# Layer 3 of a four-layer image network: reciprocal steps folded into the transform's columns, two clipping passes, and a software pipeline over quarters of a strip

## The chip, the cores and the metric

The kernel runs on one core of a Trainium2 chip. Time is device microseconds of one execution. A core has five engines that run side by side: TensorE (PE; its weight loads are shown apart as PEld), VectorE (DVE), ScalarE (ACT), GpSimd (POOL) and SyncE (SP). In this kernel SP issues every transfer, so SP's instruction stream is one queue in which a waiting transfer holds up all that stand behind it. 16 DMA engines move the data between the chip's memory (DRAM) and the on-chip buffer SBUF; PSUM is the small memory into which PE writes.

## The reference

The network adds four layers to an input x of 2 images x 64 channels x 256 x 256 pixels, each as x = x + layer(group_norm(x)). Layers 0 to 2 are an attention over 3x3 neighbours, a pair of state-space scans, and a filtered block transform with a gated convolution. The change is about layer 3:

```
def _L3_conv_ref(x, q_table, is_encoder):       # D is the 8x8 DCT matrix
    xb = x.reshape(N, C, Hb, BLOCK, Wb, BLOCK)   # 8x8 blocks
    X = jnp.einsum('ij,ncpjqk,lk->ncpiql', D, xb, D)
    X = jnp.round(X / q)
    X = jnp.clip(X, -2 ** (BIT - 1), 2 ** (BIT - 1) - 1)
    return X.reshape(N, C, H, W)
x = x + _L3_conv_ref(_gn(x), L3_conv_q_table, 1)
```

Every 8x8 block of the normalised image is transformed, each of the 64 coefficients is divided by its own entry of q, rounded, clipped to -128..127, and added to the image. All is in float32.

## The kernel before

The image lies as 128 rows (2 images x 64 channels, one per SBUF partition) of 65,536 pixels. The four layers run one after the other; each writes its result to DRAM (y0, y1, y2, then the output) and gathers the statistics for the next layer's group norm on the way. `group_norm` ends with the multiplication that writes `gnb_l` (L177); the normalisation itself, out = scale*x + shift, is done by ACT at L191.

Layer 3 works on 32 strips of 8 image rows. A strip is one megabyte, 128 x 2048 floats. For each strip:

- SP loads it into `x3s` (L1255, three buffers), and ACT normalises it into `xn` (L191), already sorted so that 16 groups of two neighbouring 8x8 blocks lie together.
- Four times, for a quarter of a strip (four groups): PE turns the four groups round with transposes into PSUM tile `pt` (L1261), ACT copies them to `xT` (L1263), PE multiplies each with the 128x128 matrix `c_dct` (L1266) into PSUM tile `pd`, and DVE multiplies `pd` by the reciprocal of q, `rq`, into a quarter of `v` (L1269). `pt` and `pd` have three buffers each, `xT` two.
- DVE clips the whole strip (L1271) and rounds it (L1272) by adding and subtracting `RND` = 1.5 * 2^23, which leaves no room for a fraction. Both run in place on 2048 floats per partition.
- POOL adds `x3s` to `v` into `y3s` (L1274, two buffers), and SP stores it (L1275).

At the head of layer 3 the matrix and q are loaded (L1240, L1242), and DVE makes `rq` from q (L1245, L1247).

What sets the order: where the text says `tc.manual_schedule(...)` each engine executes its instructions as the program writes them; layers 1 and 2 are written so. Elsewhere, and so in layer 3, a planner orders each engine's stream at compile time by its own estimate of when each instruction can start. Waits between engines, and waits for a buffer to come free, are added automatically. Buffers of a closed pool are given to the pools opened next, so a pool's first buffers lie where the pool closed just before it had its own.

`run` calls the layers in turn. Layer 2 begins with loads of its constants (L134 for `c_fwd` and `c_inv`, then L142, L851, L858, L863) and then of its first image pieces `x2s` (L881).

Of the kernel before, what the change touches and what calls it, by code (L numbers as in the profile page):

```python
# [10 lines left out]
F32 = mybir.dt.float32  # L11
BF16 = mybir.dt.bfloat16
AF = mybir.ActivationFunctionType
ALU = mybir.AluOpType
PSUM = bass.MemoryType.PSUM
DRAM = bass.MemoryType.DRAM

P = 128
C = 64
H = W = 256  # L20
# [4 lines left out]
RND = 1.5 * 2.0**23  # L25
# [95 lines left out]
class Kernel:  # L121
# [9 lines left out]
    def load(self, name, pool=None):  # L131
        ap = self.a[name]
        t = (pool or self.const).tile(list(ap.shape), F32, name=f"t_{name}", tag=f"t_{name}")
        self.nc.sync.dma_start(t, ap)  # L134
        return t
# [1095 lines left out]
        return self.group_norm("l3", stats, count[0])  # L1231


    def layer3(self, x, y, coeffs):
        nc, tc, a = self.nc, self.tc, self.a
        xv = x.rearrange("p (h w) -> p h w", w=W)
        yv = y.rearrange("p (h w) -> p h w", w=W)
        with ExitStack() as ctx:
            keep = ctx.enter_context(tc.tile_pool(name="l3k", bufs=1))
            dct = self.load("c_dct", keep)  # L1240
            q = keep.tile([P, 8, 1, 8], F32, name="q")
            nc.sync.dma_start(  # L1242
                q.rearrange("p i o l -> p (i o l)"), a["q_table"].partition_broadcast(P)
            )
            nc.vector.reciprocal(q, q)  # L1245
            rq = keep.tile([P, 8, 8, 8], F32, name="rq")
            nc.vector.tensor_copy(rq, q.to_broadcast([P, 8, 8, 8]))  # L1247
            rq = rq.rearrange("p i n l -> p i (n l)")

            pool = ctx.enter_context(tc.tile_pool(name="l3", bufs=2))  # L1250
            p_t = ctx.enter_context(tc.tile_pool(name="l3p", bufs=3, space=PSUM))
            for s in range(H // 8):
                rows = slice(8 * s, 8 * s + 8)
                xt = pool.tile([P, 8, W], F32, name="x3s", bufs=3)
                nc.sync.dma_start(xt, xv[:, rows])  # L1255
                xn = self.affine_patches(pool, "xn3", xt, coeffs)
                v = pool.tile([P, 8, W], F32, name="v3")
                for k in range(4):
                    pt = p_t.tile([P, 4, P], F32, name="pt3")
                    for g in range(4):  # L1260
                        nc.tensor.transpose(pt[:, g], xn[:, 4 * k + g], self.ident)  # L1261
                    xT = pool.tile([P, 4, P], F32, name="xT3")
                    nc.scalar.copy(xT, pt)  # L1263
                    pd = p_t.tile([P, 8, 64], F32, name="pd3")
                    for g in range(4):
                        nc.tensor.matmul(  # L1266
                            pd[:, :, 16 * g : 16 * g + 16], xT[:, g], dct, start=True, stop=True
                        )
                    nc.vector.tensor_tensor(v[:, :, 64 * k : 64 * k + 64], rq, pd, ALU.mult)  # L1269

                nc.vector.tensor_scalar(v, v, 127.0, -128.0, ALU.min, ALU.max)  # L1271
                nc.vector.tensor_scalar(v, v, RND, RND, ALU.add, ALU.subtract)  # L1272
                yt = pool.tile([P, 8, W], F32, name="y3s")
                nc.gpsimd.tensor_add(yt, v, xt)  # L1274
                nc.sync.dma_start(yv[:, rows], yt)  # L1275

    def run(self):
        x = self.a["x"]
        coeffs = self.input_stats(x)
        layers = (self.layer0, self.layer1, self.layer2, self.layer3)  # L1280
        for i, layer in enumerate(layers):
            y = self.out if i == 3 else self.scratch(f"y{i}")
            coeffs = layer(x, y, coeffs)
            x = y


@with_exitstack
# [52 lines left out]
```

## Time and profile before

| | |
|---|---|
| median of 3 runs | 19426.9 us (19423.29 to 19428.31) |
| the profiled execution: its time / its span | 19425.37 us / 19423.1 us |
| layer 1: first normalisation | 1500.7 us |
| layer 2: first transfer of `c_fwd`, first `x2s` load, first normalisation | 15725.7, 15734.2, 15738.4 us |
| `gnb_l` of layer 3 ready | 19105.8 us |
| layer 3: first normalisation; first and last addition on POOL start | 19106.0; 19126.4 and 19413.7 us |
| last addition ends / span ends | 19418.2 / 19423.1 us |

The profile is of one execution. A line such as `L1274 POOL TENSOR_TENSOR y3s<-v,x3s` names the line of the kernel, the engine, the operation and the tiles. The columns after it are explained where lines are shown. PEclk is the granted clock of TensorE as a share of full speed. Layer 3's work on the engines in its 317 us, from the groups of instructions of the last part of the trace:

| line | engine, operation | count | busy us | mean ns |
|---|---|---|---|---|
| L1261 | PE transposes | 512 | 82.3 | 306 |
| L1266 | PE products with `c_dct` (each of the 512 is two instructions) | 1024 | 147.2 | 303 |
| L191 | ACT normalise, 128x2048 | 32 | 67.1 | 2097 |
| L1263 | ACT copy, 128x512 | 128 | 71.4 | 584 |
| L1269 | DVE multiply, 128x512 | 128 | 86.0 | 683 |
| L1271 | DVE clip, 128x2048 | 32 | 75.4 | 2356 |
| L1272 | DVE round, 128x2048 | 32 | 39.1 | 1221 |
| L1274 | POOL add, 128x2048 | 32 | 144.8 | 4524 |

### The profile page before, as it was taken

Reading aid. Unit: us, or ns where it says so; the run is one execution under the profiler, and the core shown is the slowest. Engines: PE = TensorE matmul, PEld = TensorE weight load, DVE = VectorE, ACT = ScalarE, POOL = GpSimd, SP = SyncE. Lnnn points to the kernel's source line nnn. Section 1 sums busy time; section 2 is a strip of 40 time slices with the busy share of each in tenths; the row PEclk is TensorE's granted clock in tenths of the full one; section 3 lists DMA queues with packets and bytes.
Section 4 is the critical chain, followed back from the end, with each engine's and each line's share of the span. In section 5 each row is a group of like instructions: output and inputs, shape, how many; then the busy total and the mean of one; then the engine's idle time right before and its main releaser. Section 6 shows DMA issues by size and latency. Waiting matters only on the chain. (4 is left out here: it accounts for less than half of the span.)

```text
span 19423.1 us, 164029 instructions
## 1 busy us (share of the span) xinstructions
PE 14534.9 (75%) x48720; PEld 4763.2 (25%) x48720; DVE 17991.3 (93%) x15870; ACT 12151.6 (63%) x17418; POOL 16845.3 (87%) x8646
## 2 busy tenths in 40 slices
PE   7996677767777677676677677767777679999996
PEld 3441111111111111111111111111111134444444
DVE  6888999999999999999999999999999978888896
ACT  2325666666666666666666666666666657777774
POOL 5997888888888888888888888888888878888885
PEclk9996666666666666667666666666666679999997
DMA  3116666666666666666666666666666621111104
GB/s 122 57 50 150 149 156 152 150 155 149 155 150 151 156 151 152 150 150 155 152 151 154 149 156 150 150 156 151 152 150 151 154 52 32 32 32 31 32 29 147
DMA packets 662191, 2438.92 MB, mean 126 GB/s; under 512 B 131888, under 2 KB 201264, under 8 KB 450160
## 3 DMA queue, kind: packets, MB, share of 16 engines
q1 hardware_dynamic: 661296, 2428.43, 52.1%
q8 instruction: 385, 6.31, 0.1%
q14 instruction: 510, 4.18, 0.1%
HBM read 1990.14 MB, written 437.78 MB: 125 GB/s over the span
## 5 line engine op out<-in xcount | busy, mean ns | idle before, releaser
L792 DVE TENSOR_TENSOR_SCAN h<-da,st,h 128x512 f32<-128x512 f32 x8192 | 9837.9, 1262 | 310.0 <-ACT da L789 225.5
L796 POOL TENSOR_TENSOR h<-h,cb 128x2048 f32<-128x2048 f32 x2048 | 9252.4, 4518 | 164.7 <-POOL st L795 0.2
L789 ACT ACTIVATE da<-dl,p_a 128x512 f32<-128x512 f32 x8192 | 5564.3, 688 | 3976.2 <-DVE h L792 3884.3
L561 PE MATMUL py<-h,t_c_quad 128*32 128x512 f32 x16384 | 3250.7, 817 | 1649.2 <-POOL h L796 1648.3
L561 PE MATMUL pb<-bc,t_c_sel 64*128 64x512 f32 x3072 | 2696.1, 972 | 2386.6 <-DVE h L773 2381.3
L773 DVE TENSOR_TENSOR h<-dv,pb 128x2048 f32<-128x2048 f32 x1536 | 3471.5, 2260 | 40.8 <-DMA dv<-d_dv 40.8
L1023 POOL TENSOR_TENSOR gl<-gl,prod 128x512 f32<-128x512 f32 x2056 | 2606.1, 1272 | 460.9 <-ACT prod L1019 346.7
L755 POOL TENSOR_TENSOR h<-dv,cb 128x2048 f32<-128x2048 f32 x512 | 2318.7, 4529 | 16.7 <-DMA dl<-d_dl 16.7
L982 DVE SCALAR_TENSOR_TENSOR acc<-z,tap_b,acc 128x1024 f32<-128x1024 f32 (+1 forms) x1496 | 1901.6, 1271 | 22.3
L561 PEld LDWEIGHTS pb<-bc,t_c_sel 64*128 64x128 f32 x3072 | 660.9, 267 | 4410.5 <-DVE h L773 4347.0
L1019 ACT ACTIVATE prod<-z,tap_a 128x512 f32<-128x512 f32 x2056 | 1422.3, 716 | 284.8 <-POOL gl L1023 273.8
L795 POOL COPY st<-h 128x4 f32<-128x4 f32 x2048 | 383.5, 187 | 1362.9 <-DVE h L792 1331.9
L1079 PE MATMUL pcv<-z,diag 128*128 128x512 f32 x2322 | 1236.4, 642 | 179.9 <-ACT gl L1087 166.0
L561 PEld LDWEIGHTS py<-h,t_c_quad 128*32 128x32 f32 x16384 | 423.2, 122 | 3814.4 <-POOL h L796 3222.6
L561 PE MATMUL mm<-xin,p_conv 64*128 64x512 f32 x4096 | 1318.7, 773 | 15.1 <-DMA x1t<-y 15.1
L943 PE MATMUL pz<-t_c_inv,gf 128*128 128x128 f32 (+1 forms) x8192 | 964.7, 293 | 7.6 <-ACT z L951 7.3
L561 PE MATMUL mm<-u,p_dt 128*128 128x512 f32 x1024 | 929.1, 1061 | 0.0
L943 PEld LDWEIGHTS pz<-t_c_inv,gf 128*128 128x128 f32 (+1 forms) x8192 | 792.8, 170 | 484.2 <-issue 302.5
L924 DVE TENSOR_TENSOR gf<-feff,f 128x384 f32<-128x384 f32 x1024 | 558.7, 547 | 299.9 <-PE f L915 297.4
L561 PE MATMUL py<-u,p_d 128*128 128x512 f32 x1024 | 820.9, 895 | 0.0
L951 ACT COPY z<-pz 128x512 f32<-128x512 f32 x768 | 449.7, 590 | 411.1 <-PE pz L943 330.4
L561 PEld LDWEIGHTS mm<-xin,p_conv 64*128 64x128 f32 x4096 | 459.5, 244 | 980.8 <-issue 980.6
(169 smaller groups left out, 17244.8 us busy)
## 6 DMA issues: line engine op xcount, KB each, us to landing
cb<-d_bc SPq DMA_DIRECT2D x2048, 320.0 KB
dl<-d_dl SPq DMA_DIRECT2D x2048, 256.0 KB
dv<-d_dv SPq DMA_DIRECT2D x2048, 256.0 KB
d_dl<-delta SPq DMA_DIRECT2D x256, 512.0 KB
d_dv<-du SPq DMA_DIRECT2D x256, 512.0 KB
xin<-in_x SPq DMA_DIRECT2D x16, 2048.0 KB
xt<-in_x SPq DMA_DIRECT2D x32, 1024.0 KB
y<-yt SPq DMA_DIRECT2D x128, 256.0 KB
```

The source lines that it names most:

```text
L561: nc.tensor.matmul(out, lhsT, rhs, start=start, stop=stop)
L755: nc.gpsimd.tensor_tensor(h, t["dv", b], t["cb", b][:, 0].unsqueeze(1).to_broadcast([P, 4, T]), ALU.mult,)
L773: nc.vector.tensor_tensor(h, t["dv", b], pb.unsqueeze(1).to_broadcast([P, 4, T]), ALU.mult)
L789: nc.scalar.activation(da, t["dl", b][:, k], AF.Exp, scale=ws[m]["a"][:, k, j : j + 1])
L792: nc.vector.tensor_tensor_scan(h[:, k], da, h[:, k], state[m, b][:, j, k : k + 1], ALU.mult, ALU.add)
L796: nc.gpsimd.tensor_tensor(h, h, t["cb", b][:, 1 + j].unsqueeze(1).to_broadcast([P, 4, T]), ALU.mult)
L924: nc.vector.tensor_tensor(o, feff, ph[b], ALU.mult)
L943: nc.tensor.matmul(pz[i * n : (i + 1) * n, k, :, 16 * g : 16 * g + 16], gf[t, 2 * e + g, b][:, c0 : c0 + n], inv, start=True, stop=True,)
L982: eng.scalar_tensor_tensor(out, near(s, name, m0, r, k), w, box["t"], ALU.mult, ALU.add)
L1019: nc.scalar.activation(prod, near(s, name, 4 * h + m, n, k), AF.Copy, scale=w)
L1023: nc.gpsimd.tensor_add(acc, acc, prod)
L1079: nc.tensor.matmul(box["t"], diag[:, k], near(s, f"a{i}", 4 * h + m, n, k), start=k == 0, stop=k == 8,)
```

## The change

The function `layer3` is split and rewritten.

1. A new function `layer3_weights` loads `c_dct` and q, takes q's reciprocal, and multiplies it into the columns of `c_dct`. `rq` and the multiplication at L1269 go. It is called before layer 2 starts, and its matrix lives in a pool that stays open from there to the end; q lies in a pool that is closed again before layer 2 opens its own.
2. A quarter leaves PSUM by one DVE instruction that adds `RND` and takes the minimum with `RND` + 127; one more DVE instruction per strip takes the maximum with `RND` - 128 and subtracts `RND`. Two passes over `v` (L1271, L1272) become one.
3. Every engine's order is written out. In step i, PE turns quarter i round and multiplies quarter i - 2; SP loads three strips ahead; ACT normalises the next strip between the copies of quarters 1 and 2.
4. Buffers: `x3s` 3 to 5, `xT` 2 to 4, `y3s` 2 to 3, `pt` and `pd` 3 to 4 each[...].
5. The last strip's addition is cut: rows 0 to 2 on POOL, rows 3 to 7 on DVE, with a store for each.

```
+    def layer3_weights(self, keep):
+        dct = self.load("c_dct", keep)
+        with self.tc.tile_pool(name="l3w", bufs=1) as pool:
+            q = pool.tile([P, 8, 1, 8], F32, name="q")
+            nc.sync.dma_start(
+                q.rearrange("p i o l -> p (i o l)"), a["q_table"].partition_broadcast(P)
+            )
             nc.vector.reciprocal(q, q)
-            rq = keep.tile([P, 8, 8, 8], F32, name="rq")
-            nc.vector.tensor_copy(rq, q.to_broadcast([P, 8, 8, 8]))
+            columns = dct.rearrange("p (i n l) -> p i n l", n=2, l=8)
+            nc.vector.tensor_tensor(columns, columns, q.to_broadcast([P, 8, 2, 8]), ALU.mult)
+        return dct
...
-                    nc.vector.tensor_tensor(v[:, :, 64 * k : 64 * k + 64], rq, pd, ALU.mult)
-                nc.vector.tensor_scalar(v, v, 127.0, -128.0, ALU.min, ALU.max)
-                nc.vector.tensor_scalar(v, v, RND, RND, ALU.add, ALU.subtract)
-                yt = pool.tile([P, 8, W], F32, name="y3s")
-                nc.gpsimd.tensor_add(yt, v, xt)
-                nc.sync.dma_start(yv[:, rows], yt)
...
+            def load(s):
+                if s < nstrip:
+                    xt[s] = pool.tile([P, 8, W], F32, name="x3s", bufs=5)
+                    nc.sync.dma_start(xt[s], xv[:, 8 * s : 8 * s + 8])
+            def norm(s):
+                if s < nstrip:
+                    xn[s] = self.affine_patches(pool, "xn3", xt[s], coeffs)
+            def turn(s, k):
...
+                xT[s, k] = pool.tile([P, 4, P], F32, name="xT3", bufs=4)
+                nc.scalar.copy(xT[s, k], pt)
+            def transform(s, k):
...
+                nc.vector.tensor_scalar(
+                    v[s][:, :, 64 * k : 64 * k + 64], pd, RND, RND + 127.0, ALU.add, ALU.min
+                )
+            def finish(s):
+                t = v.pop(s)
+                nc.vector.tensor_scalar(t, t, RND - 128.0, RND, ALU.max, ALU.subtract)
+                yt = pool.tile([P, 8, W], F32, name="y3s", bufs=3)
+                parts = ((nc.gpsimd, 0, 8),)
+                if s + 1 == nstrip:
+                    parts = ((nc.gpsimd, 0, 3), (nc.vector, 3, 8))
+                for eng, lo, hi in parts:
+                    eng.tensor_add(yt[:, lo:hi], t[:, lo:hi], xt[s][:, lo:hi])
+                    nc.sync.dma_start(yv[:, 8 * s + lo : 8 * s + hi], yt[:, lo:hi])
+            with tc.manual_schedule(engines={E.PE, E.DVE, E.Activation, E.Pool, E.SP}):
+                for s in range(3):
+                    load(s)
+                norm(0)
+                for i in range(4 * nstrip + 2):
+                    s, k = divmod(i, 4)
+                    if s < nstrip:
+                        if k == 0:
+                            load(s + 3)
+                        turn(s, k)
+                        if k == 1:
+                            norm(s + 1)
+                    if i >= 2:
+                        s, k = divmod(i - 2, 4)
+                        transform(s, k)
+                        if k == 3:
+                            finish(s)
...
+                if i == 2:
+                    keep = ctx.enter_context(self.tc.tile_pool(name="l3k", bufs=1))
+                    dct = self.layer3_weights(keep)
+                coeffs = layer(x, y, coeffs, *([dct] if i == 3 else []))
```

More of the change, by code (lines that the diff above doesn't have):

```diff
@@ L1231, in layer2 @@
         return self.group_norm("l3", stats, count[0])
[L1234 to L1241, printed above, removed]
+    def layer3_weights(self, keep):
+        nc, a = self.nc, self.a
+        dct = self.load("c_dct", keep)
+        with self.tc.tile_pool(name="l3w", bufs=1) as pool:
+            q = pool.tile([P, 8, 1, 8], F32, name="q")
             nc.sync.dma_start(
@@ L1245, in layer3 @@
             nc.vector.reciprocal(q, q)
-            rq = keep.tile([P, 8, 8, 8], F32, name="rq")
-            nc.vector.tensor_copy(rq, q.to_broadcast([P, 8, 8, 8]))
-            rq = rq.rearrange("p i n l -> p i (n l)")
-            pool = ctx.enter_context(tc.tile_pool(name="l3", bufs=2))
[L1251 to L1268, printed above, removed]
-                    nc.vector.tensor_tensor(v[:, :, 64 * k : 64 * k + 64], rq, pd, ALU.mult)
-                nc.vector.tensor_scalar(v, v, 127.0, -128.0, ALU.min, ALU.max)
-                nc.vector.tensor_scalar(v, v, RND, RND, ALU.add, ALU.subtract)
-                yt = pool.tile([P, 8, W], F32, name="y3s")
-                nc.gpsimd.tensor_add(yt, v, xt)
-                nc.sync.dma_start(yv[:, rows], yt)
@@ new lines, in layer3_weights, with layer3 @@
+            columns = dct.rearrange("p (i n l) -> p i n l", n=2, l=8)
+            nc.vector.tensor_tensor(columns, columns, q.to_broadcast([P, 8, 2, 8]), ALU.mult)
+        return dct
+    def layer3(self, x, y, coeffs, dct):
+        nc, tc = self.nc, self.tc
+        xv = x.rearrange("p (h w) -> p h w", w=W)
+        yv = y.rearrange("p (h w) -> p h w", w=W)
+        nstrip = H // 8
+        with ExitStack() as ctx:
+            pool = ctx.enter_context(tc.tile_pool(name="l3", bufs=2))
+            p_t = ctx.enter_context(tc.tile_pool(name="l3pt", bufs=4, space=PSUM))
+            p_d = ctx.enter_context(tc.tile_pool(name="l3pd", bufs=4, space=PSUM))
+            xt, xn, xT, v = {}, {}, {}, {}
+            def load(s):
[6 more added lines that the diff above has]
+            def turn(s, k):
+                pt = p_t.tile([P, 4, P], F32, name="pt3")
+                for g in range(4):
+                    nc.tensor.transpose(pt[:, g], xn[s][:, 4 * k + g], self.ident)
+                xT[s, k] = pool.tile([P, 4, P], F32, name="xT3", bufs=4)
+                nc.scalar.copy(xT[s, k], pt)
+            def transform(s, k):
+                pd = p_d.tile([P, 8, 64], F32, name="pd3")
+                t = xT.pop((s, k))
+                for g in range(4):
+                    nc.tensor.matmul(
+                        pd[:, :, 16 * g : 16 * g + 16], t[:, g], dct, start=True, stop=True
+                    )
+                if k == 0:
+                    v[s] = pool.tile([P, 8, W], F32, name="v3")
+                nc.vector.tensor_scalar(
[11 more added lines that the diff above has]
+                    nc.sync.dma_start(yv[:, 8 * s + lo : 8 * s + hi], yt[:, lo:hi])
+            E = mybir.EngineType
+            with tc.manual_schedule(engines={E.PE, E.DVE, E.Activation, E.Pool, E.SP}):
[5 more added lines that the diff above has]
+                    if s < nstrip:
+                        if k == 0:
+                            load(s + 3)
[7 more added lines that the diff above has]
+                            finish(s)
@@ L1280, in run @@
         layers = (self.layer0, self.layer1, self.layer2, self.layer3)
[L1281 to L1284, printed above, removed]
+        with ExitStack() as ctx:
+            for i, layer in enumerate(layers):
+                y = self.out if i == 3 else self.scratch(f"y{i}")
+                if i == 2:
+                    keep = ctx.enter_context(self.tc.tile_pool(name="l3k", bufs=1))
+                    dct = self.layer3_weights(keep)
+                coeffs = layer(x, y, coeffs, *([dct] if i == 3 else []))
+                x = y
 @with_exitstack
```

## Prediction

> **What bounds the kernel now.** I first read where layer 3 lies: from `gnb_l` at 19105.8 us to the span's end at 19423.1, 317 us or 1.6% of the span, with nothing of another layer beside it, so all of it is on the path. The first addition on POOL starts at 19126.4, the last at 19413.7: 31 strips in 287.3 us, **9.27 us a strip**. Nothing in the change touches layers 0 and 1, and layer 2 only at its start.
>
> Then the chain of work that ended last, in order of time (start, duration, what):
>
> ```profile
> 19161.91 4.51 POOL y3s L1274
> ...
> 19166.87 6.86 DMA x3s<-y
> ...
> 19173.76 2.10 ACT xn L191
> ...
> 19189.78 4.51 POOL y3s L1274
> ...
> 19194.74 6.97 DMA x3s<-y
> ```
>
> The reader is to see a ring: a strip's addition frees an `x3s` buffer, the load into it takes 6.9 us because the store issued just before it goes first, then ACT, PE, DVE and POOL follow one after another. No engine is the bound; the ring is. The waits of layer 3 say the same (who waited for whom: total us, times, longest):
>
> ```profile
> POOL y3s L1274 <- DVE v L1272: 147.0, 31, 9.7
> ...
> ACT xn L191 <- DMA x3s<-y: 77.6, 23, 6.2
> ```
>
> So each resource has room, and the question is what a strip costs when the ring is opened. Stretches of 8 us, and of 1 us around one store and load (columns: length, then busy time and instructions of PE, PEld, DVE, ACT, POOL, then granted clock, DMA share, GB/s):
>
> ```profile
> 19180.00:19188.00 8.00, 7.64 (x64) 6.92 (x63) 6.55 (x8) 5.20 (x7) 4.54 (x1) 1.00 0.05 20
> ```
>
> ```profile
> 19223.00:19224.00 1.00, 0.00 (x0) 0.00 (x0) 0.97 (x2) 1.00 (x1) 0.00 (x0) 0.50 0.95 393
> 19224.00:19225.00 1.00, 0.64 (x3) 0.64 (x4) 0.60 (x1) 0.31 (x1) 0.27 (x1) 0.50 1.13 393
> 19225.00:19226.00 1.00, 1.00 (x7) 0.93 (x5) 0.00 (x0) 0.43 (x1) 1.00 (x1) 0.50 0.99 229
> 19226.00:19227.00 1.00, 1.00 (x5) 0.80 (x4) 0.00 (x0) 0.73 (x2) 1.00 (x1) 0.50 0.91 279
> 19227.00:19228.00 1.00, 1.00 (x7) 1.00 (x6) 0.00 (x0) 0.01 (x1) 1.00 (x1) 0.50 1.01 426
> 19228.00:19229.00 1.00, 1.00 (x7) 1.00 (x6) 0.61 (x1) 0.00 (x0) 1.00 (x1) 0.50 0.89 377
> ```
>
> Last, DVE's clip beside POOL (start, duration, engine):
>
> ```profile
> 19217.74 4.51 POOL L1274 TENSOR_TENSOR y3s<-v,x3s 128x2048 f32<-128x2048 f32 x1 [2.95 <-DVE v L1272]
> 19219.59 3.75 DVE L1271 TENSOR_SCALAR v<-v 128x2048 f32<-128x2048 f32 x1
> ...
> 19223.37 1.23 DVE L1272 TENSOR_SCALAR v<-v 128x2048 f32<-128x2048 f32 x1
> ```
>
> The same kind of instruction takes 1.23 us alone and 3.75 beside an addition: it ends at 19223.34, 1.09 us after POOL's end at 19222.25. A 2048-float pass on DVE waits for POOL.
>
> **The strip after the change, by resource.**
>
> PE: 512 + 1024 instructions over 32 strips are 48 a strip, unchanged. The dense stretch above has 64 in 7.64 us, 0.119 us each: 5.73 us. [...] The row is of these float32 tiles, so I take 5.73. [...]
>
> DVE: four passes out of PSUM and one over the strip. One-source copies from PSUM took 424 ns for 256 floats (L234) and 558 for 384 (L846), so 692 for 512, as L1269 took (683): fusing the rounding costs nothing there. 4 x 0.69 + 1.22 = 3.98 us, against 6.27 before (86.0 + 75.4 + 39.1 over 32). The quarter passes read PSUM, and L1269 (672 to 690 ns throughout) shows that such passes don't wait for POOL.
>
> POOL: 4.52 us, but the strip's last DVE pass cannot run beside it: 4.52 + 1.09 + 0.13 from its end to the next addition (19224.60 to 19224.73) is a loop of 5.74 us. It needs the four quarter passes, 2.8 us, to lie beneath the addition's 4.52; if that cover goes, 2.8 us come on top.
>
> ACT: 4 x 0.584 + 2.10 = 4.43 us. Normalising stands between the copies of quarters 1 and 2; while it runs, PE has a turn, two products and another turn before it needs the next copy, some 3 us for 2.1. If a load were late, the copies behind it on ACT's queue and then PE would wait for it.
>
> DMA: 2.10 MB a strip. The six slices above move 393+393+229+279+426+377 = 2097 kB in 6.0 us: store, a dip at the change to the load (229 and 279 where 400 is usual, 0.73 us lost), load. A change from load to the next store does not occur without a gap in this trace. Bounds: no dips at all, 5.2 us; a second dip, 6.7. I take 6.0, the row itself.
>
> Does SP keep DMA fed? It issues store, load, store, load; load n stands behind the store of strip n-5, which waits for POOL, and its buffer is free then. It is wanted three strips less 7 us later (addition 4.6 us, ACT's lead 2.4): 3 x 6.1 - 7 = 11 us, where a pair lands in 6.9. So no ring closes.
>
> The largest is DMA's 6.0, with PE and POOL 0.3 behind; for waits where three so nearly agree I add 0.1. **6.1 us a strip**: 31 x (9.27 - 6.1) = 98.3 us gained.
>
> **Head of layer 3.** The loads of `c_dct` and q go, and with them the reciprocal and the wait of load 1 until 19106.8. But the first buffer of the layer's pool now lies where group norm's small tiles lay, as `c_dct` did before; SP's wait for it is in the trace:
>
> ```profile
> SPq L134 <- DVE gnb_l L177: 4.9, 1, 4.9
> ```
>
> So load 0, with all other loads behind it, starts at 19105.9 instead of 19100.6. One megabyte alone lands in some 4 us (6.9 less 2.6 for the store). Normalising then runs 19110.0 to 19112.1; PE starts at half clock (a quarter's turn 0.9 us, its product 1.8), ACT's second normalisation lies between, and the fourth product ends near 19122; with the last quarter pass and the strip pass POOL starts at 19124.0: 2.4 us gained. If load 0 is not held, 6.4.
>
> **Tail.** 768 floats on POOL (1.27 us for 512, 2.36 for 1024) take 1.82, 1280 on DVE (0.69 for 512, 2.26 for 2048) 1.48. [...]
>
> ```profile
> L430 DVE TENSOR_TENSOR part<-term,part x128: 684/689/691, 208.1 to 1448.9; 128x512 f32<-128x512 f32 x128
> ```
>
> Two SBUF inputs, minimum, median and maximum equal, though POOL's products at L356 run beside it (for instance at 706.8). Side by side: 1.95 us to POOL's end instead of 4.52, 2.6 gained; by the rule 1.2. I take 2.6. The last megabyte's stores then need the same 4.95 us as now.
>
> **Layer 2's start.** `c_dct` takes over the wait for `gnb_l` (7.0 us there too), q's load comes behind it, and `c_fwd` gets the place of q, so its load waits until DVE has multiplied q into the columns. Behind it on SP stand `c_inv`, L142, L851, L858, L863 and `x2s`, for which ACT idles 21.5 us. Least: the planner puts those ahead, and only two more issues count, 0.35 + 0.42 = 0.8 us. Most: all wait; q goes out 0.4 us after `gnb_l`, lands 4.4 us later (as in layer 3, 19106.3 to 19110.7), then the reciprocal's 0.55 and some 0.3 for the product, so `c_fwd` goes 5.7 us after `gnb_l` instead of 0.1. Nothing hides it. I take 3.
>
> **Sum.** 98.3 + 2.4 + 2.6 - 3 = 100.3 us, against the profiled execution: its span 19423.1 becomes 19322.8, and with 2.3 us around it 19325.1. The median of the runs is 1.5 above the profiled time: **19327 us** (0.51% faster).
>
> **Rivals.**
>
> *Both changes of direction dip* (15%). DMA needs 6.7 us a strip: 31 x 0.6 more, 19345 us. For it: share near 1.0 during the dip, so the engines are not idle, they are slow. Against: a change from reads to writes has no row.
>
> *DVE and POOL in convoy* (7%). If PE delivers late, quarter passes fall behind the strip pass that waits for POOL, and run after it: 4.52 + 1.22 + 4 x 0.69 = 8.5 us, 31 x 2.4 more, 19401 us, about as before. For it: DVE is one queue, and the three-strip pattern of now has such waits of 2.4 to 3.75 us. Against: four `pd` buffers let PE run a strip ahead of DVE.
>
> *PE at half clock* (4%), the slower case. Place: the whole of layer 3. At clock 0.50, 16 products took 3.78 us at 19226.2, about 0.23 us each; 48 x 0.23 = 11.0 us a strip, 31 x 4.9 more, 19479 us. It decides from 9.34 us a strip, 0.195 us an instruction. For it: layers 1 and 2 have a granted clock of 0.6 to 0.7 with PE busy two thirds of the time. Against: in layer 3 it is 1.00 in dense stretches and 0.50 only after gaps of 4.5 us and more, which go.
>
> **Chances and range.** Forecast 70%: its own range has 5.75 to 6.5 us a strip, load 0 held or not, layer 2 later by 0.8 to 5.7: 19308 to 19342. Another 4% is for smaller unnamed waits, up to 8 us a strip. 0.2% is 38.9 us, about what a measurement of this kernel can tell from no change; the convoy falls inside it. Faster 0.89, same 0.07, slower 0.04. The range 19306 to 19365 (7.3 us a strip) leaves out convoy, half clock and the rest of the unnamed.
>
> **What would show it.** DMA share in layer 3 near 0.95 and 340 GB/s instead of 0.59 and 212; PE clock near 1.00; POOL starts 6.1 us apart; the strip pass at 1.2 us; first normalisation some 4 us after `gnb_l`; in layer 2 the first `x2s` load 3 us later. POOL starts 6.7 apart with DMA share 1 speak for the first rival; DVE passes of over 2 us for the second. Wrong I would be if waits for `x3s` remain on ACT.

## The result, and the profile after

| | before | after |
|---|---|---|
| median of six runs each, us | 19426.34 (19423.29 to 19428.31) | **19306.92** (19301.38 to 19307.89) |
| ratio after / before | | **0.9938**, 95% interval 0.9926 to 0.995 |
| span of the profiled execution, us | 19423.1 | 19305.7 |

The change saves 119.4 us, 0.61%. The forecast was 19327, a gain of some 100 us; the measured median lies 1 us below the forecast's own range, 19308 to 19342. The profiled executions differ by 117.4 us in their spans, and these come from four places:

| place | before | after | gained, us | predicted |
|---|---|---|---|---|
| 31 strips, from first to last POOL addition | 287.3 (9.27 each) | 178.7 (5.77 each) | **108.6** | 98.3 |
| head: `gnb_l` to first addition | 20.6 | 18.2 | 2.4 | 2.4 |
| tail: start of last addition to end | 9.4 | 8.1 | 1.3 | 2.6 |
| all before `gnb_l` of layer 3 | 19105.8 | 19100.7 | 5.1 | -3 |

The last row holds three things: layer 2's own `gnb_l` came 1.6 later, the first normalisation after it 7.8 earlier (4.9 us instead of 12.8), and the rest of layer 2 took 1.2 longer. Of these only the second is the change. In the profiles of all kernels shown here, layer 2's `gnb_l` lies between 15725.0 and 15737.1 us, and the rest of layer 2 takes 3365 to 3370 us, though nothing was edited there. So single times are not compared below some 10 us; stages are, and, as a sum, **the stretch from layer 2's `gnb_l` to the end: 3697.4 us before, 3578.5 after**, good to some 5 us. Each experiment below but the last is a single execution, and line numbers are those of its own kernel.

The chain of work that ended last, in the kernel after (start, duration, what):

```profile
19152.64 9.78 DMA x3s<-y
19162.41 0.03 issue
19162.44 2.10 ACT xn L191
...
19169.37 0.56 ACT xT L1274
19169.93 0.01 issue
19169.93 9.62 DMA x3s<-y
```

Before, an addition by POOL stood between two loads. Now the chain passes from ACT straight to the next load and never names POOL: the old ring is open. Taken at its word, it says that loads are the bound now. The timeline of POOL and DVE in the same stretch says something else (start, duration; in brackets the idle time before, and who ended it):

```profile
19199.56 4.56 POOL L1298 TENSOR_TENSOR y3s<-v,x3s 128x2048 f32<-128x2048 f32 x1 [1.22 <-DVE v L1292]
19202.46 2.75 DVE L1292 TENSOR_SCALAR v<-v 128x2048 f32<-128x2048 f32 x1
19205.33 4.56 POOL L1298 TENSOR_TENSOR y3s<-v,x3s 128x2048 f32<-128x2048 f32 x1 [1.22 <-DVE v L1292]
19207.78 3.20 DVE L1292 TENSOR_SCALAR v<-v 128x2048 f32<-128x2048 f32 x1
19211.11 4.55 POOL L1298 TENSOR_TENSOR y3s<-v,x3s 128x2048 f32<-128x2048 f32 x1 [1.22 <-DVE v L1292]
```

The strip pass of DVE starts 2.4 to 2.9 us after the addition, would take 1.2 us, and ends at 19205.21 or 19210.98: each time 1.09 us after POOL's end (19204.12, 19209.89). POOL starts 0.12 later. The addition waits for the pass, whose result it reads, and the pass for the end of the addition before, 4.55 + 1.22 = 5.77 us, strip after strip. The waits of the end of layer 2 and of layer 3 together (who for whom: total us, times, longest):

```profile
ACT xn L191 <- DMA x3s<-y: 48.7, 22, 30.4
POOL y3s L1298 <- DVE v L1292: 37.6, 31, 1.2
```

POOL waits 1.2 us at every one of 31 strips. ACT still waits for loads, 18 us in 21 waits once the longest is taken off. And 80 us of the steady part (length, then busy us and instructions of PE, PEld, DVE, ACT, POOL, then granted clock, DMA share, GB/s):

```profile
19140.00:19220.00 80.00, 75.96 (x663) 73.78 (x663) 72.46 (x71) 56.09 (x70) 62.95 (x15) 1.00 0.99 363
```

Two resources look full, DMA by its share (0.99) and PE by its busy time (95%). Neither was the bound, as the first three experiments show.

### The profile page after: what moved, and what is told of

It reads as the page before. It is cut to its first block, busy times and chain, and to the rows that moved or that the text cites. A ratio compares the mean times of both kernels' runs of the same rounds, so it can differ in the third digit from the quotient of the medians.

```text
span 19305.7 us, 164005 instructions
## 1 busy us (share of the span) xinstructions
PE 14496.9 (75%) x48720; PEld 4739.3 (25%) x48720; DVE 17967.9 (93%) x15839; ACT 12151.6 (63%) x17418; POOL 16850.4 (87%) x8646
```

## Experiments

My theory was the loop of POOL's addition and DVE's strip pass. The rivals for the 5.77 us were DMA (the forecast's own bound) and PE.

**Which of the three: no strip pass.** The last pass over the strip is left out, and with it the clip's lower half and the subtraction of `RND`.

```
-                nc.vector.tensor_scalar(t, t, RND - 128.0, RND, ALU.max, ALU.subtract)
```

> The changed kernel without the strip pass on VectorE (the maximum with RND - 128 and the subtraction of RND are left out, so the output is not the reference's). In the changed kernel POOL's additions start 5.77 us apart. Theory 1, the loop of addition and strip pass alone is the bound: without the pass the loop is 4.55 + 0.13 = 4.7 us, and the strip falls to PE's 5.32 us (what PE took per strip where it ran without a gap): 31 x 0.45 = 14 us less in layer 3, about 19293 us. Theory 2, the DMA engines are the bound as the prediction said, or stand just behind the loop: POOL's starts stay at 5.7 to 5.8 us, the time within 3 us of the changed kernel, DMA share stays at 0.99.

Additions 5.30 us apart; `gnb_l` to end 3562.6, 15.9 less. POOL's addition and the same stretch of 80 us:

```profile
19179.28 4.55 POOL L1297 TENSOR_TENSOR y3s<-v,x3s 128x2048 f32<-128x2048 f32 x1 [0.78 <-DVE v L1286]
19184.60 4.55 POOL L1297 TENSOR_TENSOR y3s<-v,x3s 128x2048 f32<-128x2048 f32 x1 [0.77 <-DVE v L1286]
```

```profile
19140.00:19220.00 80.00, 80.00 (x724) 80.00 (x723) 41.72 (x61) 61.99 (x75) 68.38 (x16) 1.00 1.00 392
```

The same transfers run at 392 GB/s, 8% faster. A DMA share of 0.99 was therefore no sign that DMA had nothing left: 363 GB/s went with 0.99, and 392 with 1.00. PE is busy 80.00 of 80 us with 724 instructions, 0.111 us each, so 48 take 5.3 us: without the pass PE is the bound.

**Less traffic instead.** Only half of each strip is stored.

```
-                    nc.sync.dma_start(yv[:, 8 * s + lo : 8 * s + hi], yt[:, lo:hi])
+                nc.sync.dma_start(yv[:, 8 * s : 8 * s + 4], yt[:, 0:4])
```

> The changed kernel with only rows 0 to 3 of each strip stored (half of the output is left unwritten): 1.57 MB a strip instead of 2.10. Theory 1, the loop of addition and strip pass is the bound: POOL's starts stay at 5.72 us (4.54 + 1.05 + 0.13, as between the first three additions of the changed kernel), the DMA share falls to about 0.75, waits for x3s on ACT go. Theory 2, DMA is the only bound: POOL's starts fall to PE's 5.32 us or below the loop's 5.72, 31 x 0.45 = 14 us less.

```profile
19140.00:19220.00 80.00, 78.10 (x688) 76.22 (x687) 78.85 (x71) 59.35 (x71) 63.72 (x14) 1.00 0.78 277
```

Still 5.765 us a strip, with the DMA share at 0.78. A quarter of the traffic is gone, and with it ACT's waits for loads (beside the layer's first one two are left, 1.1 us together, instead of 21 with 18 us), and the time per strip does not move: those waits cost nothing.

**Both.** No strip pass and half the store.

> Both of the two: no strip pass, and half of each strip stored (output not the reference's). If loop and DMA stand side by side as bounds (the first run at 5.7 or more, the second at 5.72), only both together let the strip fall to PE's 5.32 us: about 14 us less than the changed kernel, plus some 3 us from the shorter last store. If one of them alone was the bound, this run is no faster than that one's run, but for the store.

```profile
19140.00:19220.00 80.00, 80.00 (x724) 80.00 (x723) 41.63 (x61) 62.08 (x76) 68.19 (x15) 1.00 0.84 297
```

5.290 us a strip, at 297 GB/s and with PE busy throughout: the floor without the pass is the same with three quarters of the traffic, so it is PE's and not DMA's.

**What DMA alone can do.** The loop keeps only loads and stores; each strip is stored from the buffer that it was loaded into.

```
+                for s in range(nstrip):
+                    load(s + 4)
+                    nc.sync.dma_start(yv[:, 8 * s : 8 * s + 8], xt[s])
```

> Layer 3 does nothing but load each strip and store the same buffer, four loads ahead (all its computation is left out): the cost of alternating stores and loads of 1 MB without a gap, which no row of the trace before showed. The prediction took 6.0 us a pair, 5.2 without a dip at the change of direction, 6.7 with a dip at both changes. If the changed kernel's 0.99 share in 5.77 us is saturation: 5.6 to 5.75 us a pair (365 GB/s), stores issued that far apart. If DMA had room left there: near 5.2 us (400 GB/s).

Stores went out 8.75 us apart, at 241 GB/s, slower than in the full kernel. The waits of SP's queue tell why:

```profile
SPq L1262 <- DMA out<-x3s: 217.5, 27, 12.7
```

A load into a buffer waits on SP until the store out of the same buffer has landed, 217.5 us in 27 waits, and the stores behind it on SP wait too. This measures how long a store takes to land, not what DMA can move. As a measure of the rate it failed; 392 GB/s without the strip pass is the answer that it was to give.

**How the 3.5 us a strip divide: the order alone.** The written-out order and the buffers of the changed kernel, with the arithmetic of the kernel before: quarter pass times `rq`, then two strip passes. For this q stays in the pool that is kept open, and `rq` is made at layer 3's head.

```
-                    v[s][:, :, 64 * k : 64 * k + 64], pd, RND, RND + 127.0, ALU.add, ALU.min
+                nc.vector.tensor_tensor(v[s][:, :, 64 * k : 64 * k + 64], rq, pd, ALU.mult)
...
-                nc.vector.tensor_scalar(t, t, RND - 128.0, RND, ALU.max, ALU.subtract)
+                nc.vector.tensor_scalar(t, t, 127.0, -128.0, ALU.min, ALU.max)
+                nc.vector.tensor_scalar(t, t, RND, RND, ALU.add, ALU.subtract)
```

> The changed kernel's order, buffers and early weights with the arithmetic of before: multiplication by rq out of PSUM, then two passes over the strip on VectorE, both of which wait for POOL. If the loop of addition and strip passes sets the pace, it is 5.77 + 1.22 + some 0.05 = 7.0 us a strip, so 31 x 1.25 = 39 us more than the changed kernel; the order written out is then worth 9.27 - 7.0 = 2.25 us a strip (70 us) and the arithmetic 1.25 (39 us). If the second pass hides (DMA or PE the bound), it stays at 5.8 us.

7.02 us a strip, as expected. DVE's groups by line (busy us, mean ns | idle before):

```profile
L1287 DVE TENSOR_SCALAR v<-v 128x2048 f32<-128x2048 f32 x32 | 104.5, 3265 | 1.1
...
L1288 DVE TENSOR_SCALAR v<-v 128x2048 f32<-128x2048 f32 x32 | 39.3, 1227 | 1.1
```

The first of the two passes waits for POOL, the second adds its 1.23 us to the loop. So the order and the buffers are worth 9.27 - 7.02 = 2.24 us a strip, 70 us; the arithmetic 7.02 - 5.77 = 1.26, 39 us: one strip pass less in the loop.

**Layer 2's start: the weights made late.** `layer3_weights` is called inside `layer3`, as the kernel before loaded its matrix there; q lies in the same pool as the matrix.

```
-                coeffs = layer(x, y, coeffs, *([dct] if i == 3 else []))
+                coeffs = layer(x, y, coeffs)
```

> The changed kernel with c_dct and q loaded at layer 3's head, as before, instead of ahead of layer 2. From layer 2's gnb_l to its first normalisation it took 12.8 us before and 4.9 after the change. If the early load is what shortened it: 12.8 us here. In layer 3 load 0 stands behind the loads of c_dct and q, some 1 us later than in the changed kernel. Together 8 to 9 us more than the changed kernel from layer 2's gnb_l to the end (3578.6 us there).

From layer 2's `gnb_l` to its first normalisation 12.9 us again instead of 4.9; the head of layer 3 falls from 18.2 to 15.5, since `c_dct` and q now lie where group norm had its tiles and load 0 starts 5.2 us before `gnb_l`. Together 3580.9, only 2.4 more than after, where 8 to 9 were expected: 7.9 lost at layer 2's start, 2.7 gained at layer 3's head, which the expectation had as a loss, and 2.8 of drift in the rest of layer 2. So loading the weights early is worth some 5 us on balance.

**Why layer 2 starts earlier.** The first transfer of a stage into a place freed by group norm waited for `gnb_l`, in the kernel after 6.6 us on SP at layer 2's start and 5.5 at layer 3's. The question is why the first `x2s` load, which came 8.5 us after layer 2's `gnb_l`, now comes 0.9 after it. SP's queue in the kernel after:

```profile
15727.29 0.33 SPq L134 DMA_DIRECT2D t_c_dct<-in_c_dct  x1
15728.13 0.38 SPq L881 DMA_DIRECT2D x2s<-y  x1
15729.46 0.33 SPq L134 DMA_DIRECT2D t_c_fwd<-in_c_fwd  x1
```

`c_fwd` does wait for q's place, 0.9 us on SP, as predicted, but the image load stands ahead of it and not behind. The theory: the planner, which decides here what goes first on SP, counts `c_fwd` as late and so puts the image first. Then q kept to the end, and with it no wait of `c_fwd`, should bring the constants back to the front.

```
-        with self.tc.tile_pool(name="l3w", bufs=1) as pool:
-            q = pool.tile([P, 8, 1, 8], F32, name="q")
+        if True:
+            q = keep.tile([P, 8, 1, 8], F32, name="q")
```

> The changed kernel with q in the pool that stays open, so that the load of c_fwd no longer waits for VectorE's product of q and c_dct. Theory, that this wait made the planner put the first x2s load ahead of layer 2's constants: without it the constants come first again, and from gnb_l to the first normalisation it takes 12.8 + 0.8 us (two more issues), 8 to 9 us more than the changed kernel. Rival, that two more loads shift the planner's estimates anyway: x2s stays ahead, 4.9 us.

```profile
15727.16 0.35 SPq L134 DMA_DIRECT2D t_c_dct<-in_c_dct  x1
15727.56 0.43 SPq L1240 DMA_DIRECT2D q<-in_q_table  x1
15728.03 2.21 SPq L851 DMA_DIRECT2D tap_a<-in_w_dw  x4
...
15734.22 10.95 SPq L881 DMA_DIRECT2D x2s<-y  x3
```

It does: the image load comes 7.1 us after `gnb_l`, the first normalisation 6.7 us later than in the kernel after (8 to 9 were expected), and `gnb_l` to end takes 3583.9, 5.4 more than after. Taking a wait away made the stage slower, since that wait had turned the order round. The run of the order alone, which keeps q too, has the same order and 11.7 us to the first normalisation. How the planner reckons was not seen; that it counts `c_fwd` as late is inferred from these orders.

**The tail: the last addition whole on POOL.**

```
-                if s + 1 == nstrip:
-                    parts = ((nc.gpsimd, 0, 3), (nc.vector, 3, 8))
```

> The changed kernel with the last strip's addition whole on POOL. In the changed kernel it took 8.1 us from the start of the last addition to the span's end (VectorE's 1280 floats 1.49 us, POOL's 768 floats 3.05 us instead of 1.8, so POOL waited for VectorE), before 9.4. If the two exclude each other: 9.4 us here, 1.3 more. If the long addition on POOL has another cause, and cutting is worth what the prediction said: 10.7, 2.6 more.

9.5 us from the last addition's start to the end, against 8.1: the cut is worth 1.4, not 2.6. In the kernel after, the two parts:

```profile
19297.51 1.49 DVE L1298 TENSOR_TENSOR y3s<-v,x3s 128x1280 f32<-128x1280 f32 x1
19297.61 3.05 POOL L1298 TENSOR_TENSOR y3s<-v,x3s 128x768 f32<-128x768 f32 x1 [1.22 <-DVE v L1292]
```

POOL's 768 floats were to take 1.82 us; they take 3.05, ending at 19300.66, 1.66 us after DVE's end at 19299.00. One after the other, 1.49 + 1.80 us, would end at 19300.80. So they do not run side by side.

**Is it so both ways?** The same cut, with a copy out of PSUM ahead of DVE's part, so that POOL starts first.

```
+                    if lo:
+                        nc.vector.tensor_copy(pool.tile([P, 8, 64], F32, name="spare", bufs=1), last[0])
```

> The changed kernel with one unneeded copy out of PSUM (0.69 us, of a kind that never waited for POOL) on VectorE in the last strip, between the strip pass and its part of the addition, so that POOL's part of the addition starts first. So far VectorE's part started 0.1 us before POOL's and POOL lasted 1.2 us longer than its 1.82. If the two exclude each other whichever is first: POOL takes 1.8 us and VectorE's addition waits for its end, some 2.6 us instead of 1.49. If only POOL gives way (as the two-input additions of layer 0 would have it, which take 0.69 us beside POOL): VectorE's stays at 1.49 and POOL's is lengthened or not.

```profile
19294.66 0.68 DVE L1301 COPY spare<-pd 128x512 f32<-128x512 f32 x1
19294.87 1.80 POOL L1302 TENSOR_TENSOR y3s<-v,x3s 128x768 f32<-128x768 f32 x1 [1.22 <-DVE v L1294]
19295.26 2.76 DVE L1302 TENSOR_TENSOR y3s<-v,x3s 128x1280 f32<-128x1280 f32 x1
```

Now POOL takes its 1.80 us, and DVE 2.76 for what took 1.49. In both orders the first held the other up, by 1.25 and 1.27 us. The tail is 7.1 us instead of 8.1, which was not looked for. Both parts together end where they did, but POOL's, whose store stands first on SP, is done 1.25 us earlier; that its store's earlier start is what gains the 1.0 us is argued from this and not shown by a run of its own.

**A shorter loop.** The addition on POOL is cut to rows 0 to 4, and DVE adds rows 5 to 7 of every strip; each strip, the last too, has one store.

```
-                parts = ((nc.gpsimd, 0, 8),)
+                parts = ((nc.gpsimd, 0, 5), (nc.vector, 5, 8))
```

> The changed kernel with rows 5 to 7 of every strip's addition on VectorE (768 floats, some 0.95 us) and rows 0 to 4 on POOL (1280 floats, some 2.85 us alone), one store. If a VectorE instruction with two SBUF inputs and POOL exclude each other, POOL's additions last 3.8 us with VectorE's in front, and the loop is 5.0 us; if not, POOL's last 2.9. Either way the loop falls below PE's 5.32 us a strip, which then sets the pace, as in the run without the strip pass, but with the right output: 31 x 0.45 = 14 us less than the changed kernel. If DMA held the strip at 5.7 us after all, the time would stay.

```profile
19181.68 1.23 DVE L1292 TENSOR_SCALAR v<-v 128x2048 f32<-128x2048 f32 x1
19182.94 0.96 DVE L1296 TENSOR_TENSOR y3s<-v,x3s 128x768 f32<-128x768 f32 x1
...
19183.04 3.64 POOL L1296 TENSOR_TENSOR y3s<-v,x3s 128x1280 f32<-128x1280 f32 x1 [1.69 <-DVE v L1292]
```

```profile
19140.00:19220.00 80.00, 80.00 (x725) 80.00 (x724) 70.31 (x91) 62.43 (x77) 54.46 (x15) 1.00 1.01 394
```

5.32 us a strip: the strip pass takes its 1.23 us in the gap of 1.69 us between additions, and PE, busy throughout, is the bound. `gnb_l` to end 3561.7, 16.7 less than after.

**The head: a spare tile.** A tile of 1 KB per partition is allocated ahead of the pool of layer 3, so that the first `x3s` buffer no longer lies where group norm's tiles lay.

```
+            gap = ctx.enter_context(tc.tile_pool(name="l3gap", bufs=1))
+            nc.gpsimd.memset(gap.tile([P, 256], F32, name="gap"), 0.0)
```

> The changed kernel with an unused tile of 1 KB per partition ahead of layer 3's pool, so that the first x3s buffer no longer lies where group norm's small tiles were. If that place is why load 0 goes only after gnb_l: load 0 goes 5.3 us before gnb_l, the first normalisation 0.1 us after it instead of 5.0 to 5.4, and the first addition at gnb_l + 13.0 instead of 18.1 to 18.5: 5 us less from gnb_l to the end. If another wait holds load 0: no change.

In the kernel after, SP waits for `gnb_l` (total us, times, longest); with the spare tile, load 0 and four more are issued before it is ready at 19099.81 (start, duration):

```profile
SPq L1262 <- DVE gnb_l L177: 5.5, 1, 5.5
```

```profile
19094.51 2.46 SPq L1264 DMA_DIRECT2D x3s<-y  x5
```

Load 0 starts 5.3 us before `gnb_l`, and the first addition comes 12.3 us after it instead of 18.2: 5.9 us.

**Together.** Rows 5 to 7 on DVE, the spare tile, and the last strip's addition on DVE alone in two halves, each with its store.

```
-                parts = ((nc.gpsimd, 0, 8),)
+                parts = ((nc.gpsimd, 0, 5), (nc.vector, 5, 8))
                 if s + 1 == nstrip:
-                    parts = ((nc.gpsimd, 0, 3), (nc.vector, 3, 8))
+                    parts = ((nc.vector, 0, 4), (nc.vector, 4, 8))
```

> The two together, and the last strip's addition whole on VectorE in two halves with a store for each: 5.32 us a strip (14 us less), 5 us less at the head, and a tail of some 7 us instead of 8.1. About 20 us less than the changed kernel, 19287 us, ratio to the kernel before 0.9928.

Median of four runs 19286.7 us (19286.2 to 19288.5), ratio to before **0.9926** with 95% interval 0.991 to 0.9943; `gnb_l` to end 3556.3, with 5.35 us a strip. This beats both kernels: some 20 us less than the change, 142 less than before.

## Why the prediction was right or wrong

**Two terms of the sum failed**, each by some 10 us, and both gave too small a gain: the time per strip (98.3 us forecast, 108.6 measured) and layer 2's start (3 lost by the forecast, 7.8 gained). The tail, 1.3 too high, made up little of it. The parts given for the forecast's own range add to 19310 at its low end, not 19308; the measured 19306.92 lies below either.

**The ring** was read rightly. Its signs, POOL between two loads, a clock that falls to 0.50 in gaps, a DMA share of 0.59, all went: in the steady part the clock is 1.00, the share 0.99. The forecast's own test, that waits for `x3s` on ACT would prove it wrong, was a bad one: 22 remain, and half a store takes 19 of them away for no gain.

**The bound per strip** is the first step that failed: "The largest is DMA's 6.0, with PE and POOL 0.3 behind; for waits where three so nearly agree I add 0.1." The three terms, and what the runs showed:

| | predicted | measured |
|---|---|---|
| DMA | 6.0, of 5.2 to 6.7 | at most 5.3 (392 GB/s without the strip pass) |
| addition and strip pass | 5.74 | **5.77** |
| PE | 5.73 | 5.3 |
| taken | 6.1 | 5.77 |

The loop was named and sized to 0.03 us, and was the bound. DMA was taken too high because six slices of 1 us, with one pair of store and load in them, were read as a limit: 350 GB/s with the dip of 0.73 us. With loads and stores always under way the mean over 80 us is 392. Single slices of 1 us still fall to 229 (19184 to 19185 in the kernel after), and why the mean is higher was not taken apart. The DMA share in the forecast's six, 0.89 to 1.13, went with 229 to 426 GB/s and so did not say what DMA could move. With the loop's own 5.74 the sum would have been 31 x (9.27 - 5.74) = 109.4, against 108.6 measured. The margin of 0.1 had no row behind it: of three nearly equal resources the one that is a closed loop set the 5.77 us, and the other two, at most 5.3 each, hid beneath it.

**PE**: the row of 0.119 us an instruction held gaps; with PE busy all the time it is 0.111, for transposes and products together. The difference did not change the sum.

**Quarter passes** took 676 ns (692 predicted; 671 to 692 throughout), and so do not wait for POOL; the four fit beneath the addition. The line "the strip pass at 1.2 us" among the signs contradicted the loop beside it: its median is 2.81 us, since it begins beneath an addition and waits for its end.

**The head** came out at 2.4 us as predicted. The mechanism was right: load 0 waited 5.5 us for `gnb_l` on SP, and the run with the spare tile shows what that wait costs. The exact number is in part luck: the first normalisation came 5.1 us after `gnb_l`, not 4.2, and the way from there to the first addition took 13.1 us, not 14.0. Four other runs with this head (half store, q kept, last addition on POOL, POOL first) took 18.5 to 19.1 us, not 18.2.

**The tail** went the way that the forecast weighed and set aside ("2.6 gained; by the rule 1.2"): the 1.2 is what is left of 4.52 us when the two parts run one after the other, 1.82 + 1.48 = 3.3 us. DVE's and POOL's parts, each with two SBUF inputs, did not run side by side in either order: 3.05 us for POOL's 1.80 with DVE first, 2.76 for DVE's 1.49 with POOL first. The tail was worth 1.3. The row that the 2.6 rested on was misread. L430 has one SBUF input and not two, since `part` lies in PSUM (lines 294, 421 and 430 of the kernel before):

```
p_s = ctx.enter_context(tc.tile_pool(name="l0ps", bufs=1, space=PSUM))
...
part = p_s.tile([P, 2, W], F32, name="part")
...
nc.vector.tensor_add(part, term[n, name], part)
```

So its 684 to 691 ns beside POOL's L356 say nothing of additions with two SBUF inputs, and the same misreading stands in what was expected of the run with POOL first. The error was to count a row's inputs without looking up in which memory each lies.

**Layer 2's start** is the second step that failed: the wait was right, the sign wrong. `c_fwd` waits until q has been multiplied into the columns, and was sent 2.2 us after `c_dct`; up to 5.7 was allowed for, but q's load did not wait for `gnb_l` at all (it was issued at 15718.5). The case left out was a gain: that the planner, seeing the wait, would move the image load ahead of all constants. The text put "least" at 0.8 us lost; no reason excluded less, and the idle 21.5 us of ACT at that place, with all the loads of constants before the image, showed that there was something to gain: 7.8 us came.

With the measured terms the sum is 108.6 + 2.4 + 1.3 + 7.8 = 120.1 us, of which the profiles show 117.4; the rest is the drift of 1.6 and 1.2 us in what was not edited.

**The rivals** did not come. Two dips would have meant 6.7 us a strip; a convoy, quarter passes of over 2 us; half clock, 0.50 instead of 1.00 in the windows. Two readings behind the last were off. A clock of 0.6 to 0.7 holds for layer 1 (0.69 from 1500 to 15720 us, PE busy 70%), not for layer 2 (0.94 from 15740 to 19100, PE busy 90%). And a gap of 3.9 us, from 19112.5 at the head of layer 3, was followed by 0.50 too.

## What to carry to other kernels

When a ring is opened, list the loops that remain and give the longest its own time: a loop of two engines that each wait for the other is a bound although neither is busy all the time (5.77 us a strip, with POOL busy 79% and DVE 91% of 80 us), and a DMA share near 1 is none until a run with less traffic is faster (with the share down from 0.99 to 0.78 a strip still took 5.765). Before a row is taken to show that two engines run side by side, look up in the source in which memory each operand lies. An elementwise pass that cannot run beside POOL belongs in the gap between POOL's instructions, so it pays to shorten POOL's part until that gap holds it (1.23 us in 1.69, and 5.32 us a strip). Where a planner sets the order, an added wait need not cost (without that of `c_fwd` the first normalisation of layer 2 came 6.7 us later), and the first buffer of a new pool inherits the last wait of the pool that was closed before it (5.5 us at layer 3's head).

## What the hardware showed that was not expected

- Alternating stores and loads of 1 MB, with rows of 8 KB in each partition, move 392 to 394 GB/s on average over 80 us. The same share of DMA time, 0.99 to 1.01, goes with 363 and with 394 GB/s.
- DVE's 2048-float pass from SBUF to SBUF waits for POOL's addition and ends 1.09 us after it, though the pass alone takes 1.23 us. What of it overlaps the addition's end was not taken apart, and whether such a pass also holds POOL up is not shown, since POOL's next addition reads its result. For additions with two SBUF inputs on both engines it is shown in both directions, 3.05 us for 1.80 on POOL and 2.76 for 1.49 on DVE.
- POOL's addition of 1280 floats took 3.63 us with DVE's 768 floats started 0.1 us before it. Between 2.36 us for 1024 and 4.55 for 2048 one would read 2.9; the 0.7 more is about the 0.86 that DVE's part then still ran.
- PE in this layer, busy without a gap, takes 0.111 us for a 128x128 float32 transpose or half of a product with `c_dct`, at clock 1.00.
